# A binarized weight made without GpSimd and turned a step later, decay sums stored through GpSimd's queue, and one chunk's turns moved into the last output projection

## The chip, the cores and the metric

The kernel runs on one core of a Trainium2 chip. The metric is the device time of one execution in microseconds (us), lower is better. Beside it stands a profiled execution, whose span runs from the first to the last recorded instruction. Five engines matter: PE (TensorE, matmuls and transposes), DVE (VectorE), ACT (ScalarE), POOL (GpSimd) and SP (SyncE, which here only issues DMAs). Each engine works through its own queue in order and waits on semaphores. A DMA is issued from some engine's queue, and it can stand behind a waiting instruction there.

## The reference: what is computed

The input x has 4 batches of 512 tokens and 512 features, all float32. A small product of a condition vector c with w_mod gives six vectors per batch (shift, scale and gate, twice). Then two residual steps follow:

```
h = layernorm(x) * (1 + ca) + sa;   x = x + ga * mixer(h)
h = layernorm(x) * (1 + cb) + sb;   x = x + gb * (h @ bw^T + bias)
```

The mixer projects h (512) onto 1024 x channels, 512 B, 512 C, 1024 z channels and 64 step sizes dt = softplus(.). A causal convolution of width 4 and a SiLU act on x, B and C. A state space scan follows, in chunks of 128 tokens, with 64 heads of 16 channels in 8 groups of 64 states: with A_cum the running sum of -dt within a chunk, the output of a chunk is the sum over earlier tokens of (C_s . B_z) exp(A_cum_s - A_cum_z) x_z, plus C_s exp(A_cum_s) times the state carried in; the state carried on decays by exp of the chunk's total. D * x / dt is added, the whole is multiplied with SiLU(z) and projected back to 512.

The second step's weight is binarized: alpha is the mean of |w| over a row of 512, and bw = +alpha where w >= 0 and -alpha elsewhere. The reference writes it as (bw - w) + w, which is bw up to rounding.

## The kernel before

**Tiling.** The 2048 tokens are worked in 8 halves h of 256 tokens (two halves per batch), each of two chunks c of 128 tokens. A chunk's 64 heads are taken in 4 parts gp of 16 heads. So there are 64 units (h, c, gp), one per step of the main loop; 8 steps make a half. All of the weights live in SBUF.

**Stages of a unit.** `stage0` loads a unit's sums: `load_sums` (L536, L537) reads the running sums of dt from DRAM, broadcast over partitions, into a decay tile. `stage1` runs sixteen exponentials on ACT in place (L544), and DVE multiplies them with the masked scores C.B (gm, L618, and L622). `burst` makes the scores on PE (gy, L210 and L213). `stage2` multiplies the decays with the x channels on PE (py, also through `glued`, L210 and L213); DVE and POOL add the carried part and D (yt, L663 to L671) and multiply with the gate (z, L672). For the state, POOL scales x (xd, L679), PE multiplies with B (pst, L684), and POOL and DVE carry the state S (L689, L694).

**What feeds the units.** While half h is scanned, half h + 1 is prepared: layer norm, turning (`f_hT`), step sizes (`f_dt`), projections with convolution (`conv_pair`: PE L432, ACT L445, three DVE operations L449, tanh L453, L454), turning of x and B (`f_xt`, `f_Bt`). `f_dt` ends in three tiles: sh (sums), es (exponentials, ACT L389) and r (D / dt). They are stored to DRAM (`sums_d` L387, `e_d` L391, `r_d` L405) and read back broadcast: sums by `load_sums`, e by `stage0` (L577), r by `f_xt` (rr, L497), where POOL multiplies it with x (xs, L502). All these DMAs are on SP's queue.

**The tail of a chunk.** `tail1` is the output projection (po, L716, eight matmuls of 128 x 128 on 512 columns, each shown as two), gate, residual and layer norm (st_f, mv_f, rs_f with POOL's power L298, t L300). `tail2` turns t on PE (ph, L735) and applies scale and shift on ACT (h, L737). `tail3` is the product with the turned binarized weight bwT (pf, L753), gate, bias and residual (o, L755, L756) and the store (L757).

**The binarized weight.** For each of four row blocks o, `signs(o)` loads 128 rows (fw), makes alpha on DVE (L272, L273) and the signed weight (L275, L276), and POOL subtracts and adds fw (L277, L278). `turned_signs` turns it on PE (pbw, L285) and copies it from PSUM into bwT on ACT (L286).

**What sets the order.** The lists FIRST, SECOND and FRONT and the calls `at(step, ...)` say in which step of the main loop a piece is emitted; a tile scheduler places the instructions of each engine in the order of priorities, which follows from emission. `tc.issue_after(x)` holds an instruction behind x in its queue; `behind(h, f)` does this with H[h]["last"], the latest projection matmul of half h. `glued` makes the products that follow the first one keep together. PSUM tiles under the tag "mm" (projections, turns, po, ph, pf, pst and pbw among them) share five buffers, so a PE group may have to wait until the oldest of them has been read. Tiles of a tag in the pool `wk` share their buffers likewise.

Of the kernel before, what the change touches and what calls it, by code (L numbers as in the profile page):

```python
# [2 lines left out]

# [8 lines left out]
F32 = mybir.dt.float32  # L12
AF = mybir.ActivationFunctionType
ALU = mybir.AluOpType
AX = mybir.AxisListType
PSUM = bass.MemoryType.PSUM
P = 128

B, L, DM = 4, 512, 512
DI, NS, NG, NH = 1024, 64, 8, 64  # L20
# [7 lines left out]
NHALF = B * L // T  # L28
HPB = L // T
NK = DM // P  # L30
NKI = DI // P
# [8 lines left out]
def adaln_mamba_block(  # L40
# [15 lines left out]
    nc = tc.nc  # L56
# [148 lines left out]
        for v in (cw, cb, zb):  # L205
            nc.vector.tensor_scalar(v, v, 0.5, None, ALU.mult)

    def glued(products):

        first = products[0]()  # L210
        with tc.issue_after(first.ins), tc.high_priority(offset=1000):
            for product in products[1:]:
                product()  # L213
# [53 lines left out]
    def signs(o):  # L267

        fw = wk.tile([P, DM], F32, tag="h2", name=f"fw{o}")
        nc.sync.dma_start(fw, ffn_w[o * P : (o + 1) * P, :])  # L270
        alpha = wk.tile([P, 1], F32, tag="rs1", name=f"alpha{o}")
        nc.vector.tensor_reduce(alpha, fw, AX.X, ALU.add, apply_absolute_value=True)  # L272
        nc.vector.tensor_scalar(alpha, alpha, 1.0 / DM, None, ALU.mult)  # L273
        sw = wk.tile([P, DM], F32, tag="CB"[o % 2], name=f"sw{o}", bufs=3)
        nc.vector.tensor_scalar(sw, fw, 0.0, 2.0, ALU.is_ge, ALU.mult)  # L275
        nc.vector.tensor_scalar(sw, sw, -1.0, alpha, ALU.add, ALU.mult)  # L276
        nc.gpsimd.tensor_sub(sw, sw, fw)  # L277
        nc.gpsimd.tensor_add(sw, sw, fw)  # L278
        sws[o] = sw

    def turned_signs(h, o):
        sw = sws.pop(o)
        pt = ps.tile([P, NK, P], F32, tag="mm", name=f"pbw{o}")
        for i in range(NK):
            nc.tensor.transpose(pt[:, i, :], sw[:, i * P : (i + 1) * P], ident)  # L285
        nc.scalar.copy(bwT[:, :, o * P : (o + 1) * P], pt)  # L286


    def layer_norm(tiles, name, into=None):
# [63 lines left out]
    def f_dt(h):  # L353

        hT = H[h]["hT"]

        def small(tag, bufs=1):  # L360
            return wk.tile([P, CH], F32, tag=tag, name=f"{tag}_{h}", bufs=bufs)

        pa = ps.tile([P, CH], F32, tag="mm", name=f"pa_{h}")
        for k in range(NK):
            for c in range(2):
                mm(pa[c * NH : (c + 1) * NH, :], win[:, k, NCONV + DI :],
                   hT[:, k, KS - 1 + c * CH : KS - 1 + (c + 1) * CH], start=(k == 0), stop=(k == NK - 1))
        u, r, q, dt, relu = (small(n) for n in ("du", "dr", "dq", "da", "dl"))
        nc.vector.tensor_scalar(relu, pa, 0.0, None, ALU.max)
        nc.scalar.activation(u, pa, AF.Abs)  # L370
        nc.scalar.activation(u, u, AF.Exp, scale=-1.0)
        nc.vector.tensor_scalar(r, u, 2.0, None, ALU.add)
        nc.vector.reciprocal(r, r)
        nc.vector.tensor_mul(u, u, r)
        nc.vector.tensor_mul(q, u, u)
        nc.vector.tensor_scalar(dt, q, SERIES[0], None, ALU.mult)
        for cf in SERIES[1:]:
            nc.vector.scalar_tensor_tensor(dt, dt, cf, q, ALU.add, ALU.mult)
        nc.vector.scalar_tensor_tensor(dt, dt, 1.0, u, ALU.add, ALU.mult)
        nc.vector.scalar_tensor_tensor(dt, dt, 2.0, relu, ALU.mult, ALU.add)  # L380

        up = relu
        nc.vector.tensor_tensor_scan(up, ones, dt, 0.0, ALU.mult, ALU.add)
        sh = small("sh", 2)
        nc.vector.tensor_scalar(sh, up, up[:, CH // 2 - 1 : CH // 2], None, ALU.subtract)
        with tc.issue_after(last_win):
            nc.sync.dma_start(sums_d[h].rearrange("c h s -> (c h) s"), sh)  # L387
        es = small("es", 2)
        nc.scalar.activation(es, up, AF.Exp, scale=-1.0)  # L389
        with tc.issue_after(last_win):  # L390
            nc.sync.dma_start(e_d[h].rearrange("c h s -> (c h) s"), es)  # L391

        ntot = wk.tile([P, 1], F32, tag="ntot", name=f"ntot_{h}", bufs=1)
        nc.vector.tensor_scalar(ntot, up[:, CH - 1 : CH], -1.0, None, ALU.mult)
        ed = u
        nc.scalar.activation(ed, up, AF.Exp, bias=ntot)

        dg = q
        nc.vector.tensor_scalar(dg, ident, es[:, CH - 1 : CH], None, ALU.mult)

        nc.vector.reciprocal(r, dt)
        nc.vector.tensor_scalar(r, r, dsk, None, ALU.mult)
        with tc.issue_after(last_win):
            for c in range(2):
                nc.sync.dma_start(r_d[h, :, c, :], r[c * NH : (c + 1) * NH, :])  # L405
        H[h].update(turn=(sh, ed, dg))

    def first_dt(h):
# [218 lines left out]
    def stage2(h, c, gp):  # L627
# [4 lines left out]
        n = f"{h}_{c}_{gp}"  # L632
# [13 lines left out]
        for r in range(2):  # L646
            glued([
                partial(
                    mm, py[32 * j : 32 * j + 32, r, :],
                    xp[:, r * 2 * P + 32 * (2 * j + q) : r * 2 * P + 32 * (2 * j + q) + 32],  # L650
                    ets[r][:, 2 * j + q, :], start=(q == 0), stop=(q == 1),
                )
                for q in range(2) for j in range(HPG // 2)
            ])

        cs = slice(c * CH, (c + 1) * CH)
        zg = H[h]["z"][gp][:, :, cs]
# [53 lines left out]
    def tail1(h, c):  # L711
        b = h // HPB
        x2 = tails[h, c]
        po = ps.tile([P, DM], F32, tag="mm", name=f"po_{h}_{c}")
        for g in range(NKI):
            last_po = mm(po, H[h]["z"][g // 2][:, g % 2, c * CH : (c + 1) * CH], wout[:, g, :],  # L716
                         start=(g == 0), stop=(g == NKI - 1))
        t = wk.tile([P, DM], F32, tag="t", name=f"t_{h}_{c}", bufs=1)
        nc.vector.tensor_mul(t, po, gates[b][:, 0, :])
        nc.vector.tensor_add(x2, x2, t)  # L720
        layer_norm([x2], f"f{h}_{c}", [t])
        nc.gpsimd.tensor_add(x2, x2, gates[b][:, 2, :])
        tails[h, c] = (x2, t)
        if (h, c) == (NHALF - 1, 1):

            with tc.issue_after(last_po.ins):
                tail3(h, 0)

    def tail2(h, c):
        b = h // HPB  # L730
        x2, xn = tails[h, c]
        pt = ps.tile([P, NK, CH], F32, tag="mm", name=f"ph2_{h}_{c}")
        h2 = wk.tile([P, NK, CH], F32, tag="h2", name=f"h2_{h}_{c}")
        for dt in range(NK):
            nc.tensor.transpose(pt[:, dt, :], xn[:, dt * P : (dt + 1) * P], ident)  # L735
        for dt in range(NK):
            nc.scalar.activation(  # L737
                h2[:, dt, :], pt[:, dt, :], AF.Identity,
                bias=modT[:, 2, dt, b : b + 1], scale=modT[:, 3, dt, b : b + 1],
            )  # L740
        tails[h, c] = (x2, h2)

    def tail3(h, c):
        b = h // HPB
        x2, h2 = tails.pop((h, c))

        parts = 2 if (h, c) == (NHALF - 1, 1) else 1
        n = DM // parts
        for i in range(parts):
            pf = ps.tile([P, n], F32, tag="mm", name=f"pf{i}_{h}_{c}")  # L750
            cols = slice(i * n, (i + 1) * n)
            for k in range(NK):
                mm(pf, h2[:, k, :], bwT[:, k, cols], start=(k == 0), stop=(k == NK - 1))  # L753
            o = wk.tile([P, n], F32, tag="h2", name=f"o{i}_{h}_{c}")
            nc.vector.tensor_mul(o, pf, gates[b][:, 1, cols])  # L755
            nc.vector.tensor_add(o, o, x2[:, cols])  # L756
            nc.sync.dma_start(out[h * T + c * CH : h * T + (c + 1) * CH, cols], o)  # L757
# [34 lines left out]
    def at(step, f, *args):  # L792
        steps.setdefault(step, []).append((f, args))

    for h in range(NHALF):
        for step, f, args in (FIRST, SECOND)[h] if h < 2 else FRONT:
            at(max(0, h - 1) * NU + step, f, h, *args)
        if h % HPB == 0:
            at(h * NU + 3, load_gates, h // HPB)
        if h == 0:  # L800
            at(0, load_late, h)
            at(1, behind, 0, late_mods)
            at(2, load_wout)
            for o in range(NK):
                at(o // 2 + 2, signs, o)
                at(o // 2 + 4, behind, 1, turned_signs, o)
    for h in range(NHALF):
        for c in range(2):
            end = h * NU + (c + 1) * NP
            at(end - 1, load_res, h, c)  # L810

            late = {(NHALF - 1, 0): (1, 3), (NHALF - 2, 1): (0, 1, 3)}.get((h, c), (0, 1, 2))
            for tail, step in zip((tail1, tail2, tail3), late):
                at(end + step, tail, h, c)

    POST = {}
    h = NHALF - 1
# [65 lines left out]
```

## Time and profile before

| | us |
|---|---|
| time, median of 3 runs | 755.07 (753.83 to 756.47) |
| the profiled execution's own time | 755.08 |
| its span | 753.4 |
| PE busy | 713.0 (95%) |
| DVE busy | 610.8 (81%) |
| ACT busy | 520.1 (69%) |
| POOL busy | 258.5 (34%) |
| mean granted PE clock | 0.984 of full speed |

The page of a profile gives busy times by engine, the span in 40 equal slices of 18.8 us with a digit for the busy tenths (PEclk is the clock that PE was granted, in tenths), the chain of work that ended last, and groups of instructions. A group's row has line, engine, operation, output and inputs with their shapes, count, busy time and mean. A timeline row has start, length, engine, line, operation, tiles, and in brackets the time that the engine had idled before it and what ended that idling. PE is matmul, PEld the load of the stationary operand; SPq and POOLq are queues, whose DMA issues are not counted as busy. A wait row has the total, the number and the longest of the waits.

### The profile page before, as it was taken

How to read it: one execution, taken by the hardware profiler on the slowest of the kernel's cores; microseconds unless marked ns; L12 is line 12 of the kernel's file. 1: busy time of each engine (PE TensorE's matmuls, PEld its weight loads, DVE VectorE, ACT ScalarE, POOL GpSimd, SP SyncE). 2: the span in 40 equal slices, each digit the busy share in tenths (PEclk: the TensorE clock that was granted, in tenths of full speed). 3: DMA queues.
4: the chain of work that ended last, by engine and by line, in shares of the span. 5: the costliest groups of instructions: out<-in, count | busy, mean ns of one | idle time of the engine just before them, and what ended most of it. 6: DMA issues, size and time to landing. Idle time of an engine off the chain costs nothing. (4 is left out here: it accounts for less than half of the span.)

```text
span 753.4 us, 15095 instructions
## 1 busy us (share of the span) xinstructions
PE 713.0 (95%) x5196; PEld 505.6 (67%) x5196; DVE 610.8 (81%) x1226; ACT 520.1 (69%) x1503; POOL 258.5 (34%) x293
## 2 busy tenths in 40 slices
PE   6999868999999999999999999999999999999977
PEld 3786646766678666767677666786666766776643
DVE  3869888876998689976999669986898849996983
ACT  2486557749696587776777596875868758798920
POOL 4022345443143322343242341353213332334540
PEclk9999979999999999999999999999999999999989
DMA  8991583636553363424563355343634337455710
GB/s 282 313 291 42 188 193 96 166 80 144 117 142 105 84 173 105 130 68 112 142 154 105 75 142 136 113 127 90 163 89 111 93 84 182 123 161 124 161 35 28
DMA packets 121308, 99.25 MB, mean 132 GB/s; under 512 B 73984, under 2 KB 99840, under 8 KB 121232
## 3 DMA queue, kind: packets, MB, share of 16 engines
q1 hardware_dynamic: 120944, 97.76, 49.8%
q8 instruction: 41, 0.67, 0.4%
q10 hardware_dynamic: 288, 0.52, 0.2%
q14 instruction: 35, 0.29, 0.1%
HBM read 92.47 MB, written 5.79 MB: 130 GB/s over the span
## 5 line engine op out<-in xcount | busy, mean ns | idle before, releaser
L544 ACT ACTIVATE decay<-decay,st 128x128 f32<-128x128 f32 x960 | 293.3, 396 | 13.5 <-DMA decay<-sums_d 13.2
L622 DVE SCALAR_TENSOR_TENSOR decay<-decay,gm 128x1024 f32<-128x1024 f32 x120 | 155.3, 1295 | 28.3 <-ACT decay L544 26.4
L432 PE MATMUL pp_x<-hT,win 128*128 128x259 f32 x512 | 119.7, 388 | 0.0
L432 PE MATMUL pp_z<-hT,win 128*128 128x256 f32 x512 | 118.1, 383 | 0.0
L716 PE MATMUL po<-wout,z 128*128 128x512 f32 x256 | 114.2, 598 | 0.0
L679 POOL TENSOR_TENSOR xd<-xpad,st 128x256 f32<-128x256 f32 x48 | 35.0, 729 | 212.5 <-PE pst L684 161.1
L432 PEld LDWEIGHTS pp_x<-hT,win 128*128 128x128 f32 x512 | 96.2, 192 | 17.3 <-issue 2.6
L432 PEld LDWEIGHTS pp_z<-hT,win 128*128 128x128 f32 x512 | 94.3, 189 | 16.1 <-issue 3.0
L669 POOL TENSOR_TENSOR yt<-yt,xs 128x256 f32<-128x256 f32 x46 | 43.7, 950 | 128.5 <-DVE yt L668 115.9
L716 PEld LDWEIGHTS po<-wout,z 128*128 128x128 f32 x256 | 47.9, 191 | 53.8 <-issue 53.2
L449 DVE SCALAR_TENSOR_TENSOR u_x<-pp_x,cw,u_x 128x256 f32<-128x256 f32 x192 | 82.7, 474 | 0.8 <-ACT u_x L445 0.3
L213 PE MATMUL py<-decay,xpad 128*32 128x128 f32 x1680 | 68.8, 280 | 0.0
L511 ACT ACTIVATE uz<-pp_z,zb 128x256 f32<-128x256 f32 x64 | 26.8, 468 | 58.3 <-PE pp_z L432 58.3
L432 PE MATMUL pp_B<-hT,win 128*128 128x259 f32 x256 | 62.2, 395 | 0.8 <-DVE u_x L449 0.7
L672 POOL TENSOR_TENSOR z<-yt,z 128x256 f32<-128x256 f32 x62 | 57.2, 922 | 11.6 <-DVE yt L671 8.2
L502 POOL TENSOR_TENSOR xs<-u_x,rr 128x512 f32<-128x512 f32 x32 | 44.1, 1378 | 46.4 <-DVE u_x L454 38.4
L753 PE MATMUL pf<-bwT,h 128*128 128x512 f32 (+1 forms) x136 | 59.3, 576 | 0.6 <-ACT h L737 0.6
L432 PE MATMUL pp_C<-hT,win 128*128 128x259 f32 x256 | 59.5, 385 | 0.0
L445 ACT ACTIVATE u_x<-pp_x,cb,cw 128x256 f32<-128x256 f32 x64 | 35.1, 559 | 33.1 <-PE pp_x L432 32.9
L210 PE MATMUL py<-decay,xpad 128*32 128x128 f32 x240 | 48.0, 282 | 8.5 <-ACT decay L544 6.8
L432 PEld LDWEIGHTS pp_B<-hT,win 128*128 128x128 f32 x256 | 48.1, 194 | 11.2 <-DVE u_x L449 1.5
L432 PEld LDWEIGHTS pp_C<-hT,win 128*128 128x128 f32 x256 | 48.4, 192 | 7.8 <-issue 0.5
(155 smaller groups left out, 1144.5 us busy)
## 6 DMA issues: line engine op xcount, KB each, us to landing
decay<-sums_d SPq DMA_DIRECT2D x120, 256.0 KB
decay<-sums_d SPq DMA_DIRECT2D x120, 128.0 KB
rr<-r_d SPq DMA_DIRECT2D x64, 128.0 KB
e<-e_d SPq DMA_DIRECT2D x96, 64.0 KB
win<-in_w_inT SPq DMA_DIRECT2D x4, 1024.0 KB
xr<-in_x SPq DMA_DIRECT2D x16, 256.0 KB
res<-o SPq DMA_DIRECT2D x15, 256.0 KB
x<-in_x SPq DMA_DIRECT2D x14, 256.0 KB
```

Of the source, the lines that this page charges most:

```text
L210: first = products[0]()
L213: product()
L432: last = mm(pm, win[:, k, col : col + P], H[h]["hT"][:, k, lo:], start=(k == 0), stop=(k == NK - 1))
L445: nc.scalar.activation(u[:, j, :], pm[:, KS - 1 :], AF.Identity, bias=cb[:, t : t + 1], scale=cw[:, t, KS - 1 : KS])
L449: nc.vector.scalar_tensor_tensor(u[:, j, :], pm[:, k : k + T], cw[:, t, k : k + 1], u[:, j, :], ALU.mult, ALU.add)
L502: nc.gpsimd.tensor_tensor(xs, xc, rr, ALU.mult)
L544: nc.scalar.activation(ets[r][:, i, :], ets[r][:, i, :], AF.Exp, bias=H[h]["st"][:, hd : hd + 1], scale=-1.0)
L622: nc.vector.scalar_tensor_tensor(ets[r], ets[r], 1.0, bc_mid(gm[:, r, :], HPG), ALU.min, ALU.mult)
L669: ew.tensor_add(t, t, xs)
L672: ew.tensor_mul(zg, t, zg)
L716: last_po = mm(po, H[h]["z"][g // 2][:, g % 2, c * CH : (c + 1) * CH], wout[:, g, :], start=(g == 0), stop=(g == NKI - 1))
L753: mm(pf, h2[:, k, :], bwT[:, k, cols], start=(k == 0), stop=(k == NK - 1))
```

## The change

- `signs` leaves out the division of alpha by 512, L276 and both POOL operations. DVE makes +0.5 and -0.5 (`is_ge`, then subtract 0.5), and a new ACT operation multiplies with the sum of |w|, in place. The factor 2 / 512 is put into `turned_signs`' copy from PSUM, which stays on ACT.
- `turned_signs(o)` is emitted at step o // 2 + 5 instead of o // 2 + 4, and after everything else that is emitted at that step; the first chunk's `tail3` goes from two steps behind its `tail1` to three.
- The stores of sh, es and r (four DMAs per half) are issued from POOL's queue instead of SP's, except for half 0.
- The products py of the units (0, 1, gp) are placed behind the latest projection of half 1.
- At the end, `tail2` of chunk (7, 0) is no longer emitted at a step of its own but inside `tail1` of (7, 1), behind its sixth matmul step of eight. `tail1` of (7, 0) is emitted at step end + 2 instead of end + 1. The two half-width o tiles of the last chunk take buffers of the tag "th" instead of "h2".

```diff
@@ -1,4 +1,4 @@
-from contextlib import ExitStack
+from contextlib import ExitStack, nullcontext
 from functools import partial
 
 import numpy as np
@@ -205,9 +205,10 @@
         for v in (cw, cb, zb):
             nc.vector.tensor_scalar(v, v, 0.5, None, ALU.mult)
 
-    def glued(products):
-
-        first = products[0]()
+    def glued(products, after=None):
+
+        with tc.issue_after(after) if after else nullcontext():
+            first = products[0]()
         with tc.issue_after(first.ins), tc.high_priority(offset=1000):
             for product in products[1:]:
                 product()
@@ -270,12 +271,10 @@
         nc.sync.dma_start(fw, ffn_w[o * P : (o + 1) * P, :])
         alpha = wk.tile([P, 1], F32, tag="rs1", name=f"alpha{o}")
         nc.vector.tensor_reduce(alpha, fw, AX.X, ALU.add, apply_absolute_value=True)
-        nc.vector.tensor_scalar(alpha, alpha, 1.0 / DM, None, ALU.mult)
         sw = wk.tile([P, DM], F32, tag="CB"[o % 2], name=f"sw{o}", bufs=3)
-        nc.vector.tensor_scalar(sw, fw, 0.0, 2.0, ALU.is_ge, ALU.mult)
-        nc.vector.tensor_scalar(sw, sw, -1.0, alpha, ALU.add, ALU.mult)
-        nc.gpsimd.tensor_sub(sw, sw, fw)
-        nc.gpsimd.tensor_add(sw, sw, fw)
+
+        nc.vector.tensor_scalar(sw, fw, 0.0, 0.5, ALU.is_ge, ALU.subtract)
+        nc.scalar.activation(sw, sw, AF.Identity, scale=alpha)
         sws[o] = sw
 
     def turned_signs(h, o):
@@ -283,7 +282,7 @@
         pt = ps.tile([P, NK, P], F32, tag="mm", name=f"pbw{o}")
         for i in range(NK):
             nc.tensor.transpose(pt[:, i, :], sw[:, i * P : (i + 1) * P], ident)
-        nc.scalar.copy(bwT[:, :, o * P : (o + 1) * P], pt)
+        nc.scalar.activation(bwT[:, :, o * P : (o + 1) * P], pt, AF.Copy, scale=2.0 / DM)
 
 
     def layer_norm(tiles, name, into=None):
@@ -356,6 +355,8 @@
 
 
         hT = H[h]["hT"]
+
+        queue = nc.sync if h == 0 else nc.gpsimd
 
         def small(tag, bufs=1):
             return wk.tile([P, CH], F32, tag=tag, name=f"{tag}_{h}", bufs=bufs)
@@ -384,11 +385,11 @@
         sh = small("sh", 2)
         nc.vector.tensor_scalar(sh, up, up[:, CH // 2 - 1 : CH // 2], None, ALU.subtract)
         with tc.issue_after(last_win):
-            nc.sync.dma_start(sums_d[h].rearrange("c h s -> (c h) s"), sh)
+            queue.dma_start(sums_d[h].rearrange("c h s -> (c h) s"), sh)
         es = small("es", 2)
         nc.scalar.activation(es, up, AF.Exp, scale=-1.0)
         with tc.issue_after(last_win):
-            nc.sync.dma_start(e_d[h].rearrange("c h s -> (c h) s"), es)
+            queue.dma_start(e_d[h].rearrange("c h s -> (c h) s"), es)
 
         ntot = wk.tile([P, 1], F32, tag="ntot", name=f"ntot_{h}", bufs=1)
         nc.vector.tensor_scalar(ntot, up[:, CH - 1 : CH], -1.0, None, ALU.mult)
@@ -402,7 +403,7 @@
         nc.vector.tensor_scalar(r, r, dsk, None, ALU.mult)
         with tc.issue_after(last_win):
             for c in range(2):
-                nc.sync.dma_start(r_d[h, :, c, :], r[c * NH : (c + 1) * NH, :])
+                queue.dma_start(r_d[h, :, c, :], r[c * NH : (c + 1) * NH, :])
         H[h].update(turn=(sh, ed, dg))
 
     def first_dt(h):
@@ -651,7 +652,7 @@
                     ets[r][:, 2 * j + q, :], start=(q == 0), stop=(q == 1),
                 )
                 for q in range(2) for j in range(HPG // 2)
-            ])
+            ], H[1]["last"] if (h, c) == (0, 1) else None)
 
         cs = slice(c * CH, (c + 1) * CH)
         zg = H[h]["z"][gp][:, :, cs]
@@ -712,7 +713,12 @@
         b = h // HPB
         x2 = tails[h, c]
         po = ps.tile([P, DM], F32, tag="mm", name=f"po_{h}_{c}")
+        last = (h, c) == (NHALF - 1, 1)
         for g in range(NKI):
+            if last and g == NKI - 2:
+
+                with tc.issue_after(last_po.ins):
+                    tail2(h, 0)
             last_po = mm(po, H[h]["z"][g // 2][:, g % 2, c * CH : (c + 1) * CH], wout[:, g, :],
                          start=(g == 0), stop=(g == NKI - 1))
         t = wk.tile([P, DM], F32, tag="t", name=f"t_{h}_{c}", bufs=1)
@@ -721,8 +727,7 @@
         layer_norm([x2], f"f{h}_{c}", [t])
         nc.gpsimd.tensor_add(x2, x2, gates[b][:, 2, :])
         tails[h, c] = (x2, t)
-        if (h, c) == (NHALF - 1, 1):
-
+        if last:
             with tc.issue_after(last_po.ins):
                 tail3(h, 0)
 
@@ -751,7 +756,7 @@
             cols = slice(i * n, (i + 1) * n)
             for k in range(NK):
                 mm(pf, h2[:, k, :], bwT[:, k, cols], start=(k == 0), stop=(k == NK - 1))
-            o = wk.tile([P, n], F32, tag="h2", name=f"o{i}_{h}_{c}")
+            o = wk.tile([P, n], F32, tag="h2" if parts == 1 else "th", name=f"o{i}_{h}_{c}")
             nc.vector.tensor_mul(o, pf, gates[b][:, 1, cols])
             nc.vector.tensor_add(o, o, x2[:, cols])
             nc.sync.dma_start(out[h * T + c * CH : h * T + (c + 1) * CH, cols], o)
@@ -803,13 +808,14 @@
             at(2, load_wout)
             for o in range(NK):
                 at(o // 2 + 2, signs, o)
-                at(o // 2 + 4, behind, 1, turned_signs, o)
+    for o in range(NK):
+        at(o // 2 + 5, behind, 1, turned_signs, o)
     for h in range(NHALF):
         for c in range(2):
             end = h * NU + (c + 1) * NP
             at(end - 1, load_res, h, c)
 
-            late = {(NHALF - 1, 0): (1, 3), (NHALF - 2, 1): (0, 1, 3)}.get((h, c), (0, 1, 2))
+            late = {(0, 0): (0, 1, 3), (NHALF - 1, 0): (2,), (NHALF - 2, 1): (0, 1, 3)}.get((h, c), (0, 1, 2))
             for tail, step in zip((tail1, tail2, tail3), late):
                 at(end + step, tail, h, c)
 
```

## The prediction, made before the changed kernel was run

> **What bounds the kernel now.** I read the page's busy table first, then the chain, the TensorE timeline for its idle gaps, the waits, and the engines that end them.
>
> ```profile
> PE 713.0 (95%) x5196; PEld 505.6 (67%) x5196; DVE 610.8 (81%) x1226; ACT 520.1 (69%) x1503; POOL 258.5 (34%) x293
> PEclk9999979999999999999999999999999999999989
> ```
>
> TensorE (PE) is the bound: of the 753.4 us span it is idle 40.4 us (753.4 - 713.0), and several us more lie in matmuls run on a lowered clock. The matmuls themselves don't change, so a gain comes out of gaps and slow clock. PE's larger gaps, from its timeline (start, length, engine, line, tiles, idle before it):
>
> ```profile
> 99.48 1.09 PE L285 MATMUL pbw<-ident,sw 128*128 128x128 f32 x4 [7.21 <-DVE u_C L449]
> 101.92 1.11 PE L285 MATMUL pbw<-ident,sw 128*128 128x128 f32 x4 [1.35 <-POOL sw L278]
> 125.60 0.63 PE L735 MATMUL ph<-ident,t 128*128 128x128 f32 x4 [2.02 <-ACT decay L544]
> 566.37 0.27 PE L210 MATMUL py<-decay,xpad 128*32 128x128 f32 x1 [2.38 <-ACT decay L544]
> 567.15 5.20 PE L432 MATMUL pp_B<-hT,win 128*128 128x259 f32 x16
> 729.17 1.12 PE L735 MATMUL ph<-ident,t 128*128 128x128 f32 x4 [3.33 <-DVE t L300]
> 730.94 2.07 PE L716 MATMUL po<-wout,z 128*128 128x512 f32 x2
> ```
>
> After each gap of 2 us and more the same matmuls are slower: four transposes take 1.1 us against 0.60 to 0.63, sixteen projection matmuls 5.20 against 3.77, two of the output projection 2.07 against 0.88. Gaps of 1.2 us and less show no such tail.
>
> The middle gaps end on ACT's exponentials; these wait for broadcast loads, and SP, which issues the loads, stands behind the store of es. SP's timeline of the third half, and SP's own waits (total, times, longest):
>
> ```profile
> 190.31 0.34 SPq L78 DMA_DIRECT2D x<-in_x  x1
> 200.80 0.33 SPq L391 DMA_DIRECT2D e_d<-es  x1
> 203.08 0.55 SPq L536 DMA_DIRECT2D decay<-sums_d  x1
> ```
> ```profile
> SPq L391 <- ACT es L389: 66.4, 7, 10.4
> ```
> ```profile
> 207.64 2.45 ACT L544 ACTIVATE decay<-decay,st 128x128 f32<-128x128 f32 x8 [1.12 <-DMA decay<-sums_d]
> ```
>
> SP stops about 9.5 us per half until ACT has es, and the decay loads go out 2.3 us later still. GpSimd in the same stretch:
>
> ```profile
> 188.11 1.59 POOL L672 TENSOR_TENSOR z<-yt,z 128x256 f32<-128x256 f32 x1
> 205.97 0.72 POOL L669 TENSOR_TENSOR yt<-yt,xs 128x256 f32<-128x256 f32 x1 [16.27 <-DVE yt L668]
> 207.46 0.56 POOL L298 TENSOR_TENSOR rs_f<-rs_f,mhalf 128x1 f32<-128x1 f32 x1
> ```
>
> It has nothing to do for 16.27 us there.
>
> **What the Trainium skill says.** "TensorE: Matmul & The Clock Gate", Part 1 (What's actually happening): after about 3.4 us of idling the clock falls to half and about 3.4 us of work restore it. The trace agrees on the size, but shows a slow tail already after gaps of 2.02 and 2.38 us. "DMA: Bandwidth & Descriptors", SWDGE vs HWDGE vs iDMA: a DMA issued from GpSimd has its descriptors computed by that engine's own cores; and, under Anatomy of one DMA, its fixed cost is about 2.0 us, most of it the receipt of the write, with about 1 us to the first byte (Latency and other measured facts). "SBUF — State Buffer", two separate sides: VectorE operations in a 2-port mode lock GpSimd out while it writes descriptors. Nothing in the trace of before shows a data DMA from GpSimd, so these prices stay open here.
>
> **The change, part by part.**
>
> *Weight.* Four tiles each lose L276 on VectorE (0.47 to 1.48 us, 3.5 in all), L273 (0.06 apparent) and both GpSimd operations (8 of 1.27 to 2.04 us, 11 us), and gain one ACT operation of 128x512 (th_x of that shape: 0.63 us), 2.5 us in all. The transposes move a step on, behind the next projection. Before, PE's 7.21 us end when u_C's convolutions free a PSUM buffer. Two L276 (0.47 and, stretched, 1.48 us) stand ahead of them on VectorE, so what takes the buffer now (the next projection, pp_x1) starts 1.9 us earlier: idle 5.3; the slow projection behind the gap (5.18 us at 102.82 against 3.72) stays slow. The 1.35 us go. The transposes then run at full clock: 2 x 0.5 us less. The gap of 2.02 us shrinks to about 1.3 (it now ends on t of the first tail) and loses its slow tail, some 1.6 us (pp_C 4.38 against 3.72, products 0.87 against 0.50 and the like). Together 1.9 + 1.35 + 1.0 + 0.7 + 1.6 = 6.5.
>
> Against it: ACT is nearly full there. In the new order the second xpad copy (L488), which opens a pst and two PSUM buffers, stands behind one xpad copy 0.5, 32 exponentials 9.8, two weights 1.0, th_B 0.55, two turned copies 1.0, four h 1.5 and two u_C 1.0; with itself 15.9 us from 117.7, so done at 133.5. PE, 5 us earlier and with the first final product (3.6 us) moved a step on, wants it at about 130.0: 3.5 us of new idling plus about 1.5 of slow clock. Net 1.5 us gained; both ends: 6 (ACT not late) and -3 (a second wait behind the turned copies). I take 1.5.
>
> *Stores on GpSimd's queue.* 28 issues leave SP (4 in each of 7 halves). SP no longer stands still, so decay loads go at about 191 instead of 203 where their buffers are free. In even halves this removes up to 0.85 + 0.81 + 2.38 of PE idle and 1.4 of slow clock (5.20 - 3.77): 5.4. The other, smaller gaps behind the exponentials (0.92 three times in odd halves) I leave. The price is on GpSimd: it stands at es (ready at 200.77), then issues four. Queued behind are yt, z and rs_f (207.46), which t and then the transposes ph (210.38) wait for. At 1 us each they end at 205.0, before 205.97: hidden, with 1 us more of slack to ph. In odd halves es comes at 287.5; xd, at 289.66 before, goes at 291.7 and the following yt at 292.7 is just met. Bounds: 0.3 us each as on SP costs nothing; 2 us each stalls every half (below). Also r_d lands perhaps 1 us later for the rr loads; xs has slack (2.00 us of waiting for u_x, not rr, at 212.02). I take 3.5 of the 5.4.
>
> *Product glue of the second chunk behind the last projection.* It sets the place of the products of (0,1) in PE's queue behind the second half's latest projection. The first finish at 91.8, ahead of the 7.21 us gap, and VectorE uses py only at 102.00 (yt L671), behind convolutions that hide the move. Nothing; without that cover one unit's products, some 1 us, either way.
>
> *End.* The turns of chunk (7,0) move from in front of the last scores into the last output projection, between its sixth and seventh step. The gap of 3.33 us goes, with 0.62 us at 724.33 and the slow tail (0.5 on ph, 1.2 on po, 0.4 on py). Sum 6.05: PE's work from 716.64 to the last po is then 24.05 - 6.05 = 18.0 us, ending at 734.6 instead of 740.69. VectorE must keep up: without the late py its chain (t 728.57, then some eight operations of 0.42) gives the last z near 732.4, and four more matmuls of 0.44 end at 734.2, so PE still decides, by a hair. I take 5.5, bounds 4 and 6.5. The 12.7 us from the last po to the end of the span are a serial chain (t, norm, ph, h, pf, o, store) that is not touched; the o tile in another buffer removes a 2.13 us wait of VectorE at 748.51 that the chain does not pass through.
>
> Sum: 1.5 + 3.5 + 5.5 = 10.5 us against the profiled execution of 755.08 us (span 753.4, 1.7 outside), which stands at the median of 755.07. Forecast 744.5 us.
>
> **Rivals.**
>
> 1. *Only the ends pay:* GpSimd's queue is just late enough that the middle gains nothing, and ACT is late in the front. Tail 5.5, front -1, middle 0: 750.5. For it: ACT's full queue at 115 to 137 us, and only 0.9 us between the stores and yt. Against: the gaps at 213 and 566 do end on loads held up by SP.
>
> 2. *Slower: GpSimd's queue becomes the new stop.* If each store holds it for the 2 us of the skill's fixed cost, or VectorE (81% busy) starves the descriptors, even halves have GpSimd free at 209.1, so ph comes some 3 us late (three times), odd halves 1 us late (four times): 13 us lost, less 7 from front and tail: about 761. It decides from about 1.5 us per issue: (5.2 us to yt + 1 of slack)/4. Against: most of the fixed cost is the receipt, which need not hold the queue. For: GpSimd operations are visibly stretched beside VectorE (z L672: 0.73 median, 1.60 at most).
>
> 3. *More:* ACT not late, all middle gaps gone, tail 6.5: 6 + 5.4 + 6.5 = 18, with slips about 737.
>
> 4. *Nothing:* the gaps reappear one instruction later, 755. The tail speaks against it: no other engine is near PE there but VectorE.
>
> **How the numbers follow.** Within 0.3% (2.3 us) is about what a measurement of this kernel can't tell from no change. Forecast case (740 to 748.5) 0.54; ends only (748.5 to 752.8) 0.22; more (below 740) 0.09; nothing (752.8 to 757.3) 0.06; slower 0.09. So faster 0.85, same 0.06, slower 0.09. The range 738 to 753 leaves out the slower case, most of "nothing" and a little of "more".
>
> **What would show it.** Right: PE's gap before 99 us near 5.3; no idle behind pbw; a new wait of PE on ACT's xpad or bwT copies near 130 us; SP's wait on es gone and GpSimd's queue waiting on es instead; no slow projection near 566; ph for (7,0) between two po near 733, and po's last end 12.7 us before the end. Wrong: PE waiting on t, S or xd behind GpSimd's stores at each half's start (rival 2), or po waiting on z at the end, which cuts the tail's part.

## The result, and the profile after

The changed kernel takes 747.49 us (median of 4 runs, 747.10 to 747.88) against 754.45 us before (4 runs, 753.41 to 756.47): a ratio of 0.9904, 95% interval 0.9882 to 0.9927. That is 7.0 us faster. The forecast was 744.5 us in a range of 738 to 753: right in its sign and range; the time is 3 us above the forecast, a gain of 7.0 us where 10.5 were said. The profiled execution has a span of 745.9 us against 753.4.

The page's busy times and granted clock of the kernel after:

```profile
PE 711.2 (95%) x5196; PEld 503.2 (67%) x5196; DVE 602.6 (81%) x1218; ACT 523.7 (70%) x1507; POOL 260.4 (35%) x313
PEclk9999989899999999999999999999999999999999
```

PE is still busy for 95% of the span; what went is idle time, and at the end slow clock. A new slice below full clock (the eighth, 131 to 149 us) has appeared. VectorE lost 8.2 us of work, ACT got 3.6 more. PE's timeline after, at the places that the prediction named:

```profile
98.30 2.06 PE L433 MATMUL pp_x<-hT,win 128*128 128x259 f32 x4 [5.77 <-ACT decay L545]
...
121.75 0.63 PE L740 MATMUL ph<-ident,t 128*128 128x128 f32 x4 [1.38 <-ACT decay L545]
...
133.62 0.69 PE L685 MATMUL pst<-xd,bt 128*64 128x128 f32 x4 [3.20 <-ACT xpad L489]
134.24 6.25 PE L433 MATMUL pp_x<-hT,win 128*128 128x259 f32 x16
...
566.35 3.77 PE L433 MATMUL pp_B<-hT,win 128*128 128x259 f32 x16 [0.30 <-ACT st L426]
...
731.11 0.60 PE L740 MATMUL ph<-ident,t 128*128 128x128 f32 x4
731.54 1.88 PE L722 MATMUL po<-wout,z 128*128 128x512 f32 x4
```

The gap before 99 us is 5.77 us instead of 7.21, the one in front of ph 1.38 instead of 2.02. (The profile puts both down to ACT's exponentials, but VectorE's operations end there too: u_C, which frees a buffer for the one, and t, which feeds the other. In the runs a1 and a4 below the same two gaps are put down to these.) A new gap of 3.20 us stands at 133.62, in front of pst and ended by ACT's xpad copy; behind it sixteen projection matmuls take 6.25 us instead of 3.77. Near 566 us the projection runs at full clock, and ph of the last but one chunk stands between matmuls of po, without idle.

The waits of the kernel after (total, number, longest):

```profile
POOL e_d L392 <- ACT es L390: 75.8, 7, 11.8
...
ACT decay L545 <- DMA decay<-sums_d: 3.7, 6, 1.7
```

GpSimd now stands at es (75.8 us in all) as SP did before (66.4), and ACT's waiting for decay loads fell from 13.2 to 3.7 us.

Where the time went is best read from PE's own milestones: the starts of the same instruction in both traces. "Shift" is after minus before, in us.

| PE instruction | before | after | shift | what lies between this and the line above |
|---|---|---|---|---|
| turn of x, 4th | 73.24 | 73.48 | +0.24 | the start, unchanged instructions |
| turn of x, 6th | 132.73 | 126.49 | -6.24 | front: smaller gaps (two of the weight's turns not yet done: 0.9) |
| pa, half 2 | 182.91 | 183.70 | +0.79 | the stall at 133.6, its slow clock, work put off |
| pa, half 3 | 271.10 | 271.15 | +0.05 | even half: -0.7 |
| pa, half 4 | 358.68 | 360.38 | +1.70 | odd half: +1.6 |
| pa, half 5 | 446.69 | 447.83 | +1.14 | even half: -0.6 |
| pa, half 6 | 534.27 | 536.03 | +1.76 | odd half: +0.6 |
| pa, half 7 | 625.47 | 623.47 | -2.00 | even half: -3.8 |
| turn of t, (6,1) | 698.86 | 697.38 | -1.48 | odd half: +0.5 |
| turn of t, (7,1) | 744.54 | 737.28 | -7.26 | the end: -5.8 |

"Even half" here means the stretch in which half 2, 4 or 6 is prepared. Front +0.5, even -5.0, odd +2.8, end -5.8, start +0.2: -7.3. The end gains what was forecast and the even halves more; the front and the odd halves lose.

The starts differ by up to 1.7 us between runs at 73 us, where every kernel here does the same things: the first loads take differing times. In the table of the experiments "net" is the span less before's 753.4 and less this shift at 73 us. It comes from one trace per kernel, and d1 shows how far to trust it: its edit touches nothing before 200 us, and yet its front is 0.7 us longer than that of the change. The ratios compare with runs of the kernel before that were taken alongside each run; they are not quotients of the medians in this table.

### The profile page after: what moved, and what is told of

Its sections match the earlier page's. It is cut to its first block, busy times and chain, and to the rows that moved or that the text cites. A ratio compares the mean times of both kernels' runs of the same rounds, so it can differ in the third digit from the quotient of the medians.

```text
span 745.9 us, 15107 instructions
## 1 busy us (share of the span) xinstructions
PE 711.2 (95%) x5196; PEld 503.2 (67%) x5196; DVE 602.6 (81%) x1218; ACT 523.7 (70%) x1507; POOL 260.4 (35%) x313
## 3 DMA queue, kind: packets, MB, share of 16 engines
q0 software_dynamic: 896, 1.38, 0.6%
## 4 chain that ended last, share of the span: by engine, by line
PE 77%; ACT 14%; DVE 5%; issue 2%; DMA 2%; ACTq 0%; POOL 0%; SPq 0%; DVEq 0%
PE pp_x L433 16%; PE po L722 15%; PE pp_z L433 12%; ACT decay L545 10%; PE pp_B L433 7%; PE pp_C L433 7%; PE pf L758 4%; PE py L211 3%; PE py L214 3%; PE gy L211 2%; PE pt_xt L463 2%; PE pst L685 2%; PE pa L367 1%; DMA decay<-sums_d 1%; ACT h L742 1%
## 5 line engine op out<-in xcount | busy, mean ns | idle before, releaser
L433 PE MATMUL pp_x<-hT,win 128*128 128x259 f32 x512 | 122.5, 394 | 5.8 <-ACT decay L545 5.8
L433 PEld LDWEIGHTS pp_x<-hT,win 128*128 128x128 f32 x512 | 98.0, 195 | 24.1 <-ACT decay L545 6.0
L680 POOL TENSOR_TENSOR xd<-xpad,st 128x256 f32<-128x256 f32 x48 | 37.6, 784 | 188.3 <-PE pst L685 143.0
L670 POOL TENSOR_TENSOR yt<-yt,xs 128x256 f32<-128x256 f32 x46 | 41.1, 893 | 84.4 <-DVE yt L669 84.4
L214 PE MATMUL py<-decay,xpad 128*32 128x128 f32 x1680 | 67.4, 276 | 0.0
L503 POOL TENSOR_TENSOR xs<-u_x,rr 128x512 f32<-128x512 f32 x32 | 42.1, 1318 | 40.8 <-DVE u_x L455 40.8
L211 PE MATMUL py<-decay,xpad 128*32 128x128 f32 x240 | 47.5, 280 | 3.8 <-ACT decay L545 2.8
```

The source lines that it names most:

```text
L433: last = mm(pm, win[:, k, col : col + P], H[h]["hT"][:, k, lo:], start=(k == 0), stop=(k == NK - 1))
L503: nc.gpsimd.tensor_tensor(xs, xc, rr, ALU.mult)
L670: ew.tensor_add(t, t, xs)
L680: nc.gpsimd.tensor_tensor(xd, xg, by_head(H[h]["ed"][:, hd0 : hd0 + HPP]), ALU.mult)
```

## The experiments

| run | what | time, us | ratio to before (95%) | span | net |
|---|---|---|---|---|---|
| after | the change | 747.49 | 0.9904 (0.9882 to 0.9927) | 745.9 | -7.7 |
| a1 | stores back on SP | 750.09 | 0.9943 (0.9915 to 0.9971) | 748.4 | -5.0 |
| a2 | end as before | 754.77 | 0.9989 (0.9978 to 1.0001) | 752.1 | -1.4 |
| a3 | weight as before | 748.24 | 0.9907 (0.9886 to 0.9927) | 746.1 | -7.5 |
| a4 | turns and final product at old steps | 743.34 | 0.9842 (0.9820 to 0.9864) | 742.1 | -12.2 |
| b1 | one xpad copy first | 745.46 | 0.9876 (0.9852 to 0.9900) | 744.3 | -9.6 |
| b2 | no hold on products (0,1) | 748.00 | 0.9910 (0.9881 to 0.9939) | 747.7 | -6.7 |
| b3 | before, with the stores alone | 755.35 | 1.0003 (0.9989 to 1.0017) | 751.6 | -1.8 |
| c1 | stores on GpSimd in halves 2, 4, 6 | 746.67 | 0.9885 (0.9837 to 0.9933) | 744.5 | -9.7 |
| c2 | c1 and a4 | 739.53 | 0.9795 (0.9756 to 0.9834) | 737.3 | -16.5 |
| c3 | each store on GpSimd four times | 767.31 | 1.0167 (1.0124 to 1.0209) | 765.2 | +11.6 |
| c4 | turns at old steps alone | 743.02 | 0.9840 (0.9799 to 0.9881) | 742.1 | -11.3 |
| d1 | sixteen exponentials behind a tanh | 747.99 | 0.9895 (0.9873 to 0.9917) | 747.1 | -7.9 |

**a1: the stores back on SP**

```diff
-        queue = nc.sync if h == 0 else nc.gpsimd
+        queue = nc.sync
```

> The changed kernel with the stores of sums, e and r back on SP's queue in every half. Theory (the traces of before and after compared): the stores' move was worth about 2 us net, since it took 5.0 us out of the even halves (0.7 + 0.6 + 3.7) and cost some 3 us in the odd ones (0.6 to 1.6 each), where the order of the queues changed: 749.5 us, with PE idle on ACT's exponentials (0.8, 0.8, 2.4) back near 213, 390 and 566 us. Rival: the odd halves' loss comes from the weight's and tail's edits and would stay: then 5 us are lost, 752.5. Rival: GpSimd's queue costs as much as SP's wait: 747.5, no change.

Measured: 750.09 us; the net span is 2.7 us longer than after's. PE's timeline of this run has the old gaps again:

```profile
213.48 0.27 PE L211 MATMUL py<-decay,xpad 128*32 128x128 f32 x1 [1.04 <-ACT decay L545]
...
566.16 0.27 PE L211 MATMUL py<-decay,xpad 128*32 128x128 f32 x1 [2.15 <-ACT decay L545]
```

From 218 to 686 us every turn of x stands within 0.04 us of its place in the kernel before. So everything that happened between those times is due to the stores, the loss in the odd halves too: the rival that laid it to other edits falls. In total the stores' move was worth some 2.7 us. Of that 0.9 us lies at the end, which the theory did not have: there this kernel gained 4.9 us instead of 5.8, since po waits 0.42 us for GpSimd's z and 0.32 for VectorE's. In the front the stores cost something: at 152 us this run is 1.0 us ahead of the change (net of the start), of which 0.5 lie in the gap before 98 us (5.29 us here, 5.77 there).

**a2: the end as before**

```diff
-                with tc.issue_after(last_po.ins):
-                    tail2(h, 0)
+                pass
...
-            late = {..., (NHALF - 1, 0): (2,), ...
+            late = {..., (NHALF - 1, 0): (1, 3), ...
```

and the o tiles under "h2" again.

> The changed kernel with the end as before: turns of (7,0) ahead of the last scores, output projection of (7,0) a step earlier, o in the buffers of h2. Theory: the end was worth 6.0 us (3.33 + 0.62 idle and 2.1 of slow clock): 753.5, and PE idle of about 3.3 us in front of ph near 721 us. Rival: some of the 6.0 came from the steps before it: below 752.

Measured: 754.77 us, and net 6.3 us longer than after. The gap is back:

```profile
727.76 1.12 PE L739 MATMUL ph<-ident,t 128*128 128x128 f32 x4 [3.34 <-DVE t L299]
```

The end carries most of the gain. (The gap was expected at 721 us; its place in the span is 727.8.)

**a3: the weight as before.** The two functions of before, turns at o // 2 + 4 and the first final product at its old step.

> The changed kernel with the weight as before (GpSimd's subtraction and addition, VectorE's second operation, turned a step earlier, first final product at its old step). Theory: the front gave back all it gained (5.3 us gained by 126 us, 5.9 lost between 128 and 149 us by a stall on ACT and its slow clock), so that without it the time is the same or 0.5 us better: 747. Rival: the weight's edit carries part of the gain: over 749.

Measured: 748.24 us, ratio 0.9907 against 0.9904: the front's edits as a whole are worth nothing that can be measured beside the stores. The theory holds.

**a4: new arithmetic, turns and final product at their old steps**

```diff
-    for o in range(NK):
-        at(o // 2 + 5, behind, 1, turned_signs, o)
...
                 at(o // 2 + 2, signs, o)
+                at(o // 2 + 4, behind, 1, turned_signs, o)
...
-            late = {(0, 0): (0, 1, 3), ...
+            late = {...
```

> The changed kernel with the new arithmetic of the weight, but the turns at their old steps (o // 2 + 4) and the first final product two steps behind its output projection, as before. Theory (the stall near 130 us comes from the turned copies, two weights and the missing final product meeting a full ACT queue): most of the front's gain stays and the 3.2 us stall with its 2.7 us of slow clock goes, but the turns run at the lowered clock again: 743 to 745. Rival (ACT is full there whatever the turns do): 747 to 748, with the stall at another instruction.

Measured: 743.34 us, 4 us better than the change. PE's only gaps above 0.25 us between 90 and 180 us in this run:

```profile
98.98 1.08 PE L284 MATMUL pbw<-ident,sw 128*128 128x128 f32 x4 [5.76 <-DVE u_C L450]
...
123.44 0.63 PE L740 MATMUL ph<-ident,t 128*128 128x128 f32 x4 [1.65 <-DVE t L299]
```

The stall near 130 us is gone with its slow clock. (A shorter slow stretch follows the gap of 1.65 us; see the last section.) The weight's new arithmetic does pay; its later turns, or the later final product, cost that back.

**c4: which of the two moves did it?** As a4, but with the first final product three steps behind, as in the change.

> The changed kernel with the turns at their old steps, but the first final product three steps behind its output projection, as in the change. Theory (the place of the final product matters: at its old step it gives PE 3.6 us of work that needs ACT for nothing more): the stall near 130 us stays in part, 1 to 3 us, 745 to 747. Rival (the turned copies made ACT late): as with both undone, 743 to 744.

Measured: 743.02 us, net -11.3 against -12.2, and no gap near 130 us. The theory falls, the rival holds: it was the turns, not the place of the final product. That they act through their copies in ACT's queue is read from the traces (b1, next), not tested alone.

**b1: one copy in ACT's queue ahead**

```diff
-        nc.scalar.copy(
+        with tc.high_priority(offset=400) if (h, j) == (1, 1) else nullcontext():
+            nc.scalar.copy(
...
```

> The changed kernel with the second xpad copy of half 1 at a higher priority, which puts it in ACT's queue ahead of sixteen exponentials and behind three of the four h. Theory A (only the place of this copy in ACT's queue makes PE wait at pst): the 3.2 us of idle before pst at 133.6 us and the slow clock after it go, 742 to 743. Theory B (ACT is full from 118 to 134 us and every buffer that PE wants next hangs on it): pst runs some 5 us earlier, and PE waits as long one matmul group later, on u_C or the turned copies: 747 to 748.

Measured: 745.46 us, between the two theories. PE's gaps near 130 us in this run:

```profile
135.23 2.02 PE L433 MATMUL pp_x<-hT,win 128*128 128x259 f32 x8 [1.50 <-ACT bwT L285]
...
138.38 1.80 PE L433 MATMUL pp_x<-hT,win 128*128 128x259 f32 x7 [0.69 <-DVE u_C L450]
```

pst runs at 130.69, as both expected, and PE then waits for the turned copies and for u_C, as theory B had it. The two waits add up to 2.19 us where the change had 3.20, and the clock stays at 1.00 from 135 to 140 us, where it was 0.57. So the copy's place in ACT's queue was not all: most of the wait moved on to the next buffers that ACT and VectorE free, which is what a full ACT queue would do. Nearly half of the stall's price in the change was the clock (2.7 of 5.9 us). That the clock stayed up because the wait was in pieces is not shown; b2 speaks against it.

**b2: no hold on the products of (0,1).** The `after` argument of `glued` left out.

> The changed kernel without the hold of the products of units (0,1) behind half 1's latest projection. Theory, as predicted: no change, 747.5 within 1. Rival: the hold lets the projection start at 98.3 us: without it up to 2 us slower.

Measured: 748.00 us; ratio 0.9910 against 0.9904, within the intervals. Net 1.1 us longer than after, of which half is there by 152 us. The hold is worth at most a microsecond, and the times don't show it. The stall in front of pst is not in this trace; instead PE waits three times, 0.43, 0.71 and 1.90 us between 131 and 136 us, for VectorE and for ACT's exponentials, and the clock is at half from 134.11 to 140.93 us all the same.

**b3: the kernel before, with the stores alone on GpSimd**

```diff
+        queue = nc.sync if h == 0 else nc.gpsimd
...
-            nc.sync.dma_start(sums_d[h]...
+            queue.dma_start(sums_d[h]...
```

and so for e and r.

> The kernel before with only the stores moved to GpSimd's queue (halves 1 to 7). Theory: 5.0 us gained in the even halves, 3 lost in the odd ones: 752.5. Rival (the odd halves' loss belongs to the other edits): 749.5. Rival (in the first halves GpSimd is still busy with the weight and the queue hurts there): 755 or more.

Measured: 755.35 us, a ratio of 1.0003 within 0.14%: no gain in the times, where the theory had some 2.5 us; of the three only the last rival had 755 or more. Its profiled execution, one of the shorter ones of its twelve (753.39 us), is 1.8 us shorter than before's, with the pattern of the table again: even halves -0.7, -0.6 and -3.8, odd halves +1.5, +0.5 and +0.5. So the trace bears out the pattern; that the stores alone gain is not shown. The loss in the front that the last rival named is there too: PE's gap in front of the weight's turns is 8.86 us instead of 7.21, of which 0.2 us are left by 152 us.

**c1: stores on GpSimd in halves 2, 4 and 6 only**

```diff
-        queue = nc.sync if h == 0 else nc.gpsimd
+        queue = nc.gpsimd if h in (2, 4, 6) else nc.sync
```

> The changed kernel with the stores on GpSimd's queue only in halves 2, 4 and 6, and on SP's in the others. Theory (the loss of 0.6 to 1.6 us in the odd halves comes with the stores there, since ACT's queue then has exponentials ahead of a tanh): the odd halves run as before the change and the even ones keep their gain: 3.0 us off the span, 744.5. Rival (an odd half only takes up the gain of the even one in front of it, the order being set by something later): 747 to 748.

Measured: 746.67 us, net 2.0 us shorter than after; the times alone would not tell it from the change (0.9885 within 0.5%). The shifts do: by the milestones of the table the preparation of halves 5 and 7 loses 0.0 us where the change lost 0.6 and 0.5, and that of half 3 loses 0.3 instead of 1.6. The even gain stays (-0.6, -0.6, -3.8). So the loss in an odd half comes, all but 0.3 us, with the stores in that half. The missing 0.9 us are those at the end that a1 showed: with half 7's stores on SP, po waits for z again. The stall in the front is nearly as long as in the change (3.12 us).

**c2: both**

> The last one with the turns and the first final product at their old steps too. Theory: the two gains add up: 740.5. Rival: they share the same slack on ACT: 743.

Measured: 739.53 us, ratio 0.9795 (0.9756 to 0.9834), the best of all: 15 us faster than before, 8 us than the change. The two gains more than add up (net -16.5, from -12.2 and -9.7 where the change has -7.7): PE reaches 152 us 3.4 us earlier than in a4. In c2 the stores of half 1 are on SP, and PE's gaps near 98 and 121 us are 5.29 and 0.75 us instead of 5.76 and 1.65. That is 1.4 of the 3.4 us. The rest is mostly the clock: a4 has 3.41 us at half clock behind its gap of 1.65 us, c2 none there. In c1, where the stall on ACT still stands behind it, the same edit gained at most 0.8 us by 152 us.

**c3: sixteen stores instead of four**

```diff
+        def spare(i, src):
+            if h > 0:
+                for k in range(3):
+                    nc.gpsimd.dma_start(spare_d[k, h, i, : src.shape[0], :], src)
...
+            spare(0, es)
```

and so for sums and r.

> The changed kernel, each of its stores on GpSimd's queue followed by three more of the same data to a spare place in DRAM. This makes work that nobody uses. The four issues of a half took 2.24 us; sixteen take 9. Theory (GpSimd's queue has about 3 us of room in front of yt and some 4 us in front of the turns of t): 3 us late in each even half, less in odd ones, with r landing later in front of the loads on SP: 755 to 765, with PE idle in front of ph on VectorE's t. Rival (the room is larger than the trace says, all of it hidden): 747 to 749.

Measured: 767.31 us, slower by 1.67% and 2 us above the theory's range. GpSimd's timeline near the third half, and VectorE's:

```profile
200.99 0.63 POOL L399 DMA_DIRECT2D e_d<-es  x1 [11.37 <-ACT es L397]
...
208.32 1.64 POOL L365 DMA_DIRECT2D spare_d<-dr  x3 [0.40 <-DMA spare_d<-sh]
209.98 0.59 POOL L298 TENSOR_TENSOR rs_f<-rs_f,mhalf 128x1 f32<-128x1 f32 x1
```
```profile
210.60 0.94 DVE L300 TENSOR_SCALAR t<-xr,mv_f,rs_f 128x512 f32<-128x512 f32 x1 [2.24 <-POOL rs_f L298]
```

The sixteen issues hold GpSimd from 200.99 to 209.96 us. rs_f comes some 2.5 us late against PE's own work, VectorE stands at t, and behind t in its queue are the convolutions that PE's buffers wait for: PE idles 2.26 us in front of the turns of B, not in front of ph. SP also waits 37.0 us in all for r to land, with the decay loads behind it. The limit that the prediction's slower rival set (about 6 us of stores per half) lies between what was harmless to that path, 2.24 us, and these 9 us, which were not. The odd halves lost more than the even ones (+3.7, +2.4 and +3.3 us against +2.6, +1.0 and +2.5), which the theory did not have; that the waiting for r made it dearer is likely, not tested.

**d1: what an odd half loses.** In the change, ACT's queue near 305 us has this order, and before it had the other:

```profile
305.32 0.69 ACT L545 ACTIVATE decay<-decay,st 128x128 f32<-128x128 f32 x2 [1.68 <-DMA decay<-sums_d]
305.92 0.61 ACT L454 ACTIVATE th_x<-u_x 128x512 f32<-128x512 f32 x1
306.44 1.84 ACT L545 ACTIVATE decay<-decay,st 128x128 f32<-128x128 f32 x6
```
```profile
303.71 0.64 ACT L453 ACTIVATE th_x<-u_x 128x512 f32<-128x512 f32 x1
304.44 2.45 ACT L544 ACTIVATE decay<-decay,st 128x128 f32<-128x128 f32 x8
```

The tanh stands behind two exponentials that wait for their load. VectorE then waits for the tanh, and PE for VectorE:

```profile
306.56 0.69 DVE L455 SCALAR_TENSOR_TENSOR u_x<-th_x,u_x 128x512 f32<-128x512 f32 x1 [1.61 <-ACT th_x L454]
```
```profile
310.24 0.63 PE L463 MATMUL pt_xt<-ident,u_x 128*128 128x128 f32 x4 [0.85 <-DVE u_B L450]
```

The edit holds the unit's exponentials back:

```diff
+        H[h]["th", name] = nc.scalar.activation(th, u, AF.Tanh).ins
...
+                hold = (c, gp) == (1, 3) and h in (2, 4, 6)
+                with tc.issue_after(H[h + 1]["th", "x1"]) if hold else nullcontext():
...
```

> The changed kernel with the sixteen exponentials of the units (2,1,3), (4,1,3) and (6,1,3) held in ACT's queue behind the tanh of the next half's second x pair, as they stood before the change. Nothing else is held. Theory (in the odd halves a tanh stands behind two exponentials that wait 1.68 us for their load, which makes VectorE and then PE late): the loss between 304 and 327 us, 1.45 us in the profiled span, and those near 481 and 657 us, 0.4 and 0.3, go: span 743.8, time 745.5. Rival (the loss is from PE's own order, the scores ahead of the turns at 308 us, or the exponentials are then late for the products): span 745.5 to 746.5.

Measured: 747.99 us, ratio 0.9895 against 0.9904, so the times show no change; net 0.2 us shorter than after, which is within what two traces differ by. In the half in question the expected thing happened: from 244 to 327 us the loss is 0.55 us instead of 1.63, and the gap of 0.85 us is gone.

```profile
307.66 0.62 ACT L454 ACTIVATE th_x<-u_x 128x512 f32<-128x512 f32 x1
308.18 4.78 ACT L547 ACTIVATE decay<-decay,st 128x128 f32<-128x128 f32 x16
```

In the two later odd halves nothing moved (0.5 and 0.7 us), and this run's front was 0.7 us longer. So the order in ACT's queue explains two thirds of the one large loss (1.1 of 1.6 us), and neither the rest of it nor the others. c1 shows that 2.5 of the 2.8 us come with the stores in odd halves; through what the last 0.5 us per half come is open.

## Why the prediction was right and wrong

**The front (forecast 1.5 us gained; 0.5 lost).** The places were met: gap 5.77 us where 5.3 was said, 1.38 where 1.3, the stall on ACT's second xpad copy 3.20 us at 133.6 where 3.5 at 133.5. The sizes were not. Up to 126 us the shift was 6.5 us net of the start, as forecast, but 0.9 of it were turns put off, so that 5.6 were gained. Half of what is missing is a term that the prediction put at nothing, the stores of half 1. They hold GpSimd until 95.71 us, so that its xd, which ran at 92.44 in a1, comes at 95.73, and VectorE's B beside it takes 1.10 us instead of 0.67. The first two lines are from the change, the third from a1:

```profile
95.73 0.69 POOL L680 TENSOR_TENSOR xd<-xpad,st 128x256 f32<-128x256 f32 x1
95.88 1.10 DVE L455 SCALAR_TENSOR_TENSOR B<-th_B,u_B 128x512 f32<-128x512 f32 x1
```
```profile
95.57 0.67 DVE L455 SCALAR_TENSOR_TENSOR B<-th_B,u_B 128x512 f32<-128x512 f32 x1
```

With these stores on SP (a1, c1 and c2) the gap is 5.29 us, the forecast 5.3. The second mis-sized term is "about 1.5 of slow clock" behind the stall: 2.5 us in the projection (6.25 against 3.77) and 0.25 in pst. It fits the runs a1, c1 and c3, where the projection behind the same stall takes 5.01 to 5.16 us; the last section says why the clock's part is not fixed. The step that was missing is a choice: the prediction saw that ACT was full and that the turned copies were among what filled it, and a4 and c4 show that the later turns alone cost some 4 us.

**The stores (forecast 3.5; 2.3 in the trace from 184 to 686 us and 0.9 at the end, less the 0.5 in the front).** The even halves gained 5.0 of the 5.4 us that could be had, so the cut to 3.5 was made at the wrong place. The way there was not the forecast one: the decay loads, said to go "at about 191 instead of 203", went at 202.62 instead of 203.08.

```profile
202.62 0.49 SPq L537 DMA_DIRECT2D decay<-sums_d  x1
```
```profile
SPq L537 <- PE py L214: 282.6, 50, 12.7
```

SP no longer waits for es, but it waits for PE's products instead, which still read the decay tiles that these loads are to fill (282.6 us in all, 208.1 before). Measured against PE's own work, which runs 0.8 to 1.8 us later here, the loads of the three even halves go 1.0 to 1.7 us earlier, and the last one of half 6, which stood back until 558.25 us before, 3.2 us. That was enough for gaps of 0.85, 0.81 and 2.38 us. It was luck that the gaps were no longer. GpSimd's queue was overpriced: its timeline after, near the third half (h = 2), shows four issues in 2.24 us, not 4.

```profile
201.85 0.63 POOL L392 DMA_DIRECT2D e_d<-es  x1 [11.36 <-ACT es L390]
202.48 0.55 POOL L388 DMA_DIRECT2D sums_d<-sh  x1
203.02 1.06 POOL L406 DMA_DIRECT2D r_d<-dr  x2
206.76 0.73 POOL L670 TENSOR_TENSOR yt<-yt,xs 128x256 f32<-128x256 f32 x1 [2.68 <-DVE yt L669]
```

yt still waits for VectorE, not for the stores. The step that failed in sign is the odd halves: "the following yt at 292.7 is just met". That was right (yt at 292.64, xd at 289.97), and yet 2.8 us were lost there. The prediction followed GpSimd's queue and never compared ACT's, where the order of exponentials and tanh had changed with the same edit; d1 lays 1.1 of the 2.8 us to that order, and the rest is open.

**The hold on products (forecast nothing).** Right within a microsecond (b2).

**The end (forecast 5.5; 5.8 in the trace, 6.3 by a2).** Right in its steps: PE's work from the first po to the last takes 18.0 us (715.39 to 733.42) where 18.0 was said, without a gap or a slow clock.

**The rivals.** That only the ends pay came as close in time (750.5, 3 us too long) as the forecast (744.5, 3 us too short), but not in its reasons: the middle paid. The forecast is better in its mechanisms (the end, the stall on ACT), not in its number. The slower rival did not come, since an issue holds GpSimd for 0.56 us on average, a third of the 1.5 us from which it decides; c3 shows that a queue held for 9 us does cost time. The 2.0 us per DMA of the Trainium skill ("DMA: Bandwidth & Descriptors", Anatomy of one DMA) show up as the time to landing, 1.9 us for e and 1.8 for sums at the median, not as time of the queue. The lock of GpSimd by VectorE ("SBUF — State Buffer", two separate sides) is tested by no run here; the issues of e, the longest, take 0.63 us at the median and 0.77 at most.

## What to carry to other kernels

When an edit moves a DMA to another queue, compare the order of every engine's queue before and after, not only of the two queues: here ACT's order changed as well, and in one half that took back 1.1 us. Freeing a queue moves its next instruction only as far as the next wait: ask what that one is, here the buffers that PE still read. Before moving work to an engine that the trace shows full in that stretch, add up its queue there to the instruction that the bound engine needs, and price the slow clock behind a stall with the stall, as a range. A part that measures as zero may be a gain and a loss: undoing one half of the weight's edit gained 4 us, and with the stores kept to the even halves the kernel is 8 us faster than the change.

## What was not expected of the hardware

A store of 64 KB issued from GpSimd holds its queue for 0.55 to 0.77 us and lands after 1.8 to 1.9 us at the median (7.0 at most); one of 32 KB of r holds it 0.53 us and lands after 3.5 us at the median, as measured behind the two others.

Where operations of VectorE and GpSimd overlap, one or the other is longer. VectorE's B takes 0.67 us in a1 with GpSimd idle, 1.10 us beside xd in the change, and 1.75 us in b3 beside GpSimd's work on the weight, where 0.41 us on sw also become 2.01. In the kernel before it is GpSimd that loses: B keeps its 0.68 us, and the subtraction beside it takes 2.04 us instead of 1.27.

The length of a gap does not fix the slow clock behind it. From 90 us on TensorE runs at either full or half clock in these traces, and each stretch at half clock that their end doesn't cut lasts 3.41 us or two or three times that. Within a trace they start whole multiples of 3.41 us apart (before: 95.64, 126.36, 566.68 and 727.10 us). Much the same idling was followed by different stretches:

| runs | PE idle, us | half clock behind it, us |
|---|---|---|
| after, a2, d1 | 3.19 to 3.20 | 6.83 |
| a1, c1, c3 | 3.12 to 3.19 | 3.41 |
| b2 | 0.43, 0.71 and 1.90 | 6.83 |
| b1 | 1.50 and 0.69 | none |
| a4 | 1.65 | 3.41 |
| c4 | 1.65 | none |
| c3, at 667.61 us | 2.64 | none |

The same projection behind the same gap of 1.65 us, in a4 and then in c4:

```profile
126.42 4.30 PE L433 MATMUL pp_C<-hT,win 128*128 128x259 f32 x16
```
```profile
125.45 3.77 PE L433 MATMUL pp_C<-hT,win 128*128 128x259 f32 x16
```

So the prediction's reading, a slow tail after every gap of 2 us and more and none after 1.2 us and less, fits the trace of before but is no rule. It would fit that the clock is decided once in 3.41 us, so that it matters where in that period a gap falls, which differs between executions; no run here was made to test that.
